# A graph attention network on one core: a third of the columns summed on TensorE, ScalarE three rows ahead, a new order of products and tiles

## The chip, the cores and the metric

The kernel runs on one core of one Trainium2 chip. The metric is the device time of one execution in microseconds; the kernel before took 6460.51 us, the median of three runs (6455.24 to 6466.45). A core has five engines that each work through their own queue in order and wait for each other by semaphores: TensorE (PE; PEld are its weight loads), VectorE (DVE), ScalarE (ACT), GpSimd (POOL) and SyncE (SP). Bulk data moves by DMA, started from a queue of SP, ACT or POOL.

## The reference, cut to what matters

There are 10000 nodes with 768 features and 170000 edges (80000 random pairs in both directions and a loop at each node), sorted by destination. Two layers of graph attention are computed, with 4 heads of 256 columns in the first and one head of 768 columns in the second:

```python
xl = (x @ W).reshape(n, heads, out_ch)
e = leaky_relu(alpha_src[src] + alpha_dst[dst], 0.2)
e = exp(e - segment_max(e, dst)[dst])
alpha = e / (segment_sum(e, dst)[dst] + 1e-16)
out = segment_sum(xl[src] * alpha[:, :, None], dst)
```

The kernel adds a loop of its own at every node, as the reference does. After layer 1: h1 = relu(layer_norm(out)) + x @ Wr1 + br1. After layer 2: h = layer_norm(out2) + h1 @ Wr2 + br2, and the result is layer_norm(x + h). All is float32.

## The kernel before, in words

**Preparation** (0 to 958 us). The rows x @ W1, with the two attention terms of each head appended, go to `table1` in DRAM, 1032 numbers a row. Beside that, `prepare` sorts the nodes by their number of in-edges and groups them into 79 tiles of 128 nodes. Tile t gets `SLOTS[t]` slots a node (its own row, then its in-edges, filled up with a row that has no weight). `slot_counts` (L54) fixes these numbers from a formula on the numbers of nodes and edges alone: 42 for tile 0, then 28, 27, 26, down to 11. `slots` holds the row number of each slot, and `FIRST[t]` is where tile t begins.

**The ring.** In both layers a tile is worked on slot by slot. `Ring` (L380) is a buffer in SBUF of 28 slots in layer 1 and 40 in layer 2; a slot holds one row of the table for each of the 128 nodes. `fetch` (L388) issues one indirect DMA from GpSimd for each slot, through `gather` (L364). It is called after each slot that was used, so that a slot is filled again as soon as it is free. A tile with more slots than the ring (the 42-slot tile alone) goes through `attend_parts` (L442) in three parts.

**Weights.** `logits` (L403) adds the terms, applies the leaky ReLU (L169), subtracts the maximum (L413, L416) and takes the exponential on ScalarE (L417). `normalised` (L420 to L426) divides by the sum.

**Layer 1** (`ordered_layer1`, L581), for each tile: logits; the statistics of the tile before (`deviation`: L473, L475 on VectorE, the square root at L477 on ScalarE); normalising; then ScalarE builds eight diagonal matrices from the weights of the first two slots (L619) and TensorE multiplies these slots' rows by them (L625), which starts the sum `acc` in PSUM. VectorE finishes h of the tile before (`scaled`: L483 to L485, and L635). TensorE transposes h (L491, copied out by ScalarE, L494). The remaining slots are added by `weigh`: of every three, the first is multiplied and added by VectorE alone (L439, four instructions of 256 columns), and the other two are multiplied in place by ScalarE (L433, four instructions) and added by VectorE (L435, 1024 columns). At fixed slots of this loop the larger products are issued (`dense`: h times W2 with its two attention columns, the product that becomes a row of `table2`, then x times Wr1), and near its end ScalarE copies the finished row (L651) and TensorE transposes x of the next tile. GpSimd then scatters the row to `table2` (L675). hT is stored to DRAM by SyncE (L643). Products and transposes share two PSUM buffers, `ps_big`, of two banks each; `acc` has two of its own.

**Layer 2** (`ordered_layer2`, L683), for each tile: `deviation` and `scaled` for the tile before, logits, the residual added (L722), normalising, a second `deviation`; then TensorE computes the residual x + h1 @ Wr2 of this tile (L740 with the identity, L742), and VectorE adds all slots over all 768 columns (L439). `finish` (L730 to L733) gives the last norm at the third slot, and GpSimd scatters the result (L758). hT and x of tile t+2 are asked for at the end of tile t (L704 on SyncE's queue, L364 on GpSimd's).

The order of each engine's instructions is the order of the program text; nothing reorders them (`tc.manual_schedule()`).

Of the kernel before, what the change touches and what calls it, by code (L numbers as in the profile page):

```python
# [41 lines left out]
G = 4  # L42
RING1 = 28
RING2 = 40
ON_PE1 = 2
# [8 lines left out]
def slot_counts(n_nodes, n_edges):  # L54
# [8 lines left out]
    for t in range(-(-n_nodes // P)):  # L63
        room = t * P if t else 0.002
        k = next((k for k, m in enumerate(tails) if m + 4.0 * math.sqrt(m) * (t > 0) <= room), DEGREES - 3)
        counts.append(min(k + 1, DEGREES - 2))
# [4 lines left out]
def gnn_kernel(ctx, tc, x, x_cols, src, dst, src_col, dst_col, W1, a_src1, a_dst1, b1, g1, be1, Wr1, br1,  # L71
# [13 lines left out]
    FIRST = [sum(SLOTS[:t]) for t in range(NT)]  # L85
# [12 lines left out]
    ps_big = ctx.enter_context(tc.tile_pool(name="ps_big", bufs=2, space=PSUM))  # L98
    ps_tr = None

    @contextmanager
    def psum_for_transposes():

        nonlocal ps_tr
        with tc.tile_pool(name="ps_tr", bufs=2, space=PSUM) as ps_tr:
            yield
# [8 lines left out]
    slots = consts.tile([P, FIRST[-1] + SLOTS[-1]], I32, name="slots")  # L115
# [29 lines left out]
    def product(aT, w, n):  # L145

        k = w.shape[1]
        p = ps_big.tile([P, 2 * BANK], F32, name="big")
# [231 lines left out]
    class Ring:  # L380
# [6 lines left out]
        def fetch(self, upto):  # L387
            for q in range(self.issued, min(upto, FIRST[-1] + SLOTS[-1])):  # L388
                gather(self.slot(q), self.table[:, :], slots[:, q:q + 1])
                self.issued = q + 1  # L390
# [36 lines left out]

    def weigh(acc, row, e, dh, first=None, shared=False):

        if shared:  # L430
            for h in range(e.shape[1]):
                s = slice(h * dh, (h + 1) * dh)
                nc.scalar.activation(row[:, s], row[:, s], AF.Copy, scale=e[:, h:h + 1])  # L433
# [8 lines left out]
    def attend_parts(small, ring, acc, h_, ad, bias, heads, dh, t):  # L442
# [6 lines left out]
        for lo, hi in zip(cuts, cuts[1:]):  # L449
# [13 lines left out]
            for q in range(lo, hi):  # L463
                weigh(acc, ring.slot(q), e[:, q - lo], dh, shared=heads > 1 and (q - lo) % 3)
# [48 lines left out]
    with tc.tile_pool(name="w1", bufs=1) as w1p, tc.tile_pool(name="l1", bufs=2) as io, \  # L513
            psum_for_transposes(), tc.manual_schedule():
# [65 lines left out]

    def ordered_layer1():  # L581
        with tc.tile_pool(name="b1", bufs=1) as pool, tc.tile_pool(name="small1", bufs=2) as small, \
                tc.tile_pool(name="ps_acc1", bufs=2, space=PSUM) as ps_acc, tc.manual_schedule():
            ring = Ring(pool, table1, R1, RING1)
            ring.fetch(RING1)

            def fetch_x(t):
                xt = pool.tile([P, D0], F32, name="xt", bufs=2)
                gather(xt, x[:, :], order[:, t:t + 1])
                return xt  # L590

            xs = {t: fetch_x(t) for t in range(min(2, NT))}
            g1_b, be1_b = (spread(pool, v, n) for v, n in ((g1, "g1"), (be1, "be1")))

            def transposed_x(t):
                to = pool.tile([P, K0, P], F32, name="xT", bufs=2)
                return to, columns(to, xs[t])

            xT, moves = transposed_x(0)
            last = None  # L600
            for t in range(NT + 1):
                live, events = t < NT, []
                whole = live and SLOTS[t] <= ring.size
                n = SLOTS[t] if live else 0
                if live:
                    acc = ps_acc.tile([P, 2 * BANK], F32, name="acc")
                if whole:
                    ad = ring.slot(FIRST[t])[:, C1 + H1:]
                    e, _ = logits(small, ring, FIRST[t], FIRST[t] + n, ad, H1, C1)
                if last:  # L610
                    h, r, mean_rows = last
                    stats = deviation(small, mean_rows, C1)
                if whole:
                    normalised(small, e, H1)

                    diagonals = pool.tile([P, ON_PE1 * H1, P], F32, name="diagonals")
                    for k in range(ON_PE1):
                        for i in range(H1):
# [415 lines left out]
```

## Time and profile before

| what | value |
|---|---|
| median of 3 runs | 6460.51 us (6455.24 to 6466.45) |
| the profiled execution | 6474.16 us, its span 6472.3 us |
| mean granted TensorE clock | 0.819 |
| busy, whole span | PE 65%, PEld 35%, DVE 78%, ACT 42%, POOL 55% |
| gathers into the ring (L364) | 2940, mean 949 ns on POOL |
| layer 2 rows on VectorE (L439, 768 columns) | 1392, mean 1022 ns |
| layer 1 rows on VectorE alone (L439, 256 columns) | 1856, mean 490 ns |
| layer 1 rows multiplied by ScalarE (L433) | 3400, mean 500 ns |
| and added by VectorE (L435, 1024 columns) | 850, mean 1233 ns |
| moved by DMA | 1666 MB, mean 257 GB/s |

The profile is of one execution. Its page gives the busy time of each engine; a view by stretches splits that by time; the timeline lists an engine's instructions with their start, their duration and, in brackets, the idle time before them and what ended it. Three stages can be told apart: preparation until 958 us, layer 1 until the first gather of layer 2 at 3974 us, and layer 2 until the end. VectorE's last row of layer 1 ends at 3942 us; between that and 3974 us lie the last tile's h, its product, its row and the scatter to `table2`. In layer 2 VectorE begins its work on tiles at 4034 us, and its first tile (42 slots) lasts until 4095 us; its last row ends at 6452 us.

### The profile page before, as it was taken

The page shows a single profiled execution, that of the slowest core. Times are in us where ns is not written, and L with a number is a line of the kernel's source. Part 1 is how long each engine was busy: PE and PEld are TensorE (multiplying, and loading weights), DVE is VectorE, ACT ScalarE, POOL GpSimd, SP SyncE. Part 2 cuts the span into 40 slices and gives each one's busy share as a digit, 9 for nine tenths or more (in the row PEclk, how much of TensorE's full clock was granted, in tenths as well). Part 3 has the DMA queues.
Part 4 walks back from the last instruction along what each step waited for, and adds up shares of the span by engine and source line. Part 5 has one row for each costly group of instructions (what it writes and reads, how often), then busy time and mean ns, then how long its engine had stood idle before and what let it go on. Part 6 is the DMA issues. An engine that isn't in the chain of part 4 may idle for free. (4 is left out here: it accounts for less than half of the span.)

```text
span 6472.3 us, 48744 instructions
## 1 busy us (share of the span) xinstructions
PE 4198.2 (65%) x11636; PEld 2278.5 (35%) x11636; DVE 5053.9 (78%) x8160; ACT 2688.0 (42%) x6591; POOL 3534.4 (55%) x3582
## 2 busy tenths in 40 slices
PE   8997982556766777778888996333434444445555
PEld 3443431333434444444455553111212222222332
DVE  5861426888888888888888884888878888888888
ACT  3433434666666666667666772011111111111111
POOL 3426534555555555555555553666666666666663
PEclk9999996778888888889899998666667777777777
DMA  4323237888888888888888885888878888888884
GB/s 140 122 76 70 93 106 287 289 293 315 299 301 301 303 304 297 300 295 299 293 299 307 308 312 180 277 281 288 281 272 287 282 280 281 279 286 283 279 291 161
DMA packets 459455, 1666.17 MB, mean 257 GB/s; under 512 B 105739, under 2 KB 109899, under 8 KB 459158
## 3 DMA queue, kind: packets, MB, share of 16 engines
q0 software_dynamic: 362176, 1486.59, 66.6%
q1 hardware_dynamic: 93168, 170.98, 7.8%
q10 hardware_dynamic: 3814, 5.39, 0.3%
q8 instruction: 94, 1.54, 0.1%
q14 instruction: 203, 1.66, 0.1%
HBM read 1516.88 MB, written 146.19 MB: 257 GB/s over the span
## 5 line engine op out<-in xcount | busy, mean ns | idle before, releaser
L364 POOL DMA_INDIRECT ring<-table,slots x2940 | 2789.2, 949 | 2161.4 <-DVE acc L439 889.7
L439 DVE SCALAR_TENSOR_TENSOR acc<-ring,e,acc 128x256 f32<-128x256 f32 (+1 forms) x3248 | 2332.4, 718 | 363.5 <-PE acc L625 201.5
L433 ACT ACTIVATE ring<-ring,e 128x256 f32<-128x256 f32 x3400 | 1390.8, 500 | 0.0
L435 DVE TENSOR_TENSOR acc<-acc,ring 128x1024 f32<-128x1024 f32 x850 | 1048.0, 1233 | 91.9 <-ACT ring L433 2.6
L740 PE MATMUL big<-wr,ident 128*128 128x512 f32 (+1 forms) x316 | 206.7, 745 | 1280.2 <-DMA wr<-in_x_dram,order 633.2
L742 PE MATMUL big<-w,wr 128*128 128x512 f32 (+1 forms) x2528 | 950.4, 531 | 23.1 <-issue 23.0
L625 PE MATMUL acc<-ring,diagonals 128*128 128x256 f32 x1248 | 424.3, 514 | 698.9 <-ACT diagonals L619 586.8
L152 PE MATMUL big<-w,hT 128*128 128x512 f32 (+1 forms) x2528 | 840.2, 490 | 56.8 <-ACT hT L494 56.8
L152 PE MATMUL big<-w,xT 128*128 128x512 f32 x1896 | 833.4, 601 | 55.8 <-DMA xT<-in_x_cols_dram 34.7
L152 PE MATMUL big<-wr,xT 128*128 128x512 f32 x1896 | 829.5, 594 | 0.7 <-ACT xT L494 0.7
L742 PEld LDWEIGHTS big<-w,wr 128*128 128x128 f32 x2528 | 531.3, 210 | 468.1 <-issue 432.6
L477 ACT ACTIVATE sd<-mv,eps 128x1 f32<-128x1 f32 x237 | 69.7, 294 | 1358.1 <-issue 585.4
L152 PEld LDWEIGHTS big<-w,hT 128*128 128x128 f32 x2528 | 471.9, 189 | 411.8 <-issue 289.1
L625 PEld LDWEIGHTS acc<-ring,diagonals 128*128 128x128 f32 x1248 | 326.9, 269 | 782.7 <-ACT diagonals L619 598.2
L152 PEld LDWEIGHTS big<-w,xT 128*128 128x128 f32 x1896 | 363.3, 193 | 522.9 <-issue 501.8
L740 PEld LDWEIGHTS big<-wr,ident 128*128 128x128 f32 x316 | 69.7, 249 | 1349.3 <-issue 449.3
L152 PEld LDWEIGHTS big<-wr,xT 128*128 128x128 f32 x1896 | 360.8, 190 | 423.4 <-issue 417.7
L417 ACT ACT_TABLE_LOAD x156 | 200.1, 1283 | 717.7 <-DVE e L416 636.7
L569 DVE TENSOR_TENSOR scr<-big,as_b 128x1024 f32<-128x1024 f32 x79 | 96.7, 1224 | 441.2 <-ACT row L566 426.3
L574 POOL TENSOR_TENSOR row<-row,none 128x1024 f32<-128x1024 f32 x79 | 187.0, 2368 | 334.9 <-ACT row L566 334.3
L572 ACT ACTIVATE scr<-scr 128x256 f32<-128x256 f32 x632 | 253.4, 402 | 122.2 <-DVE scr L569 118.3
L477 ACT ACT_TABLE_LOAD x157 | 201.4, 1283 | 229.7 <-DVE mv L475 149.5
(146 smaller groups left out, 3359.3 us busy)
## 6 DMA issues: line engine op xcount, KB each, us to landing
ring<-table,slots POOLq DMA_INDIRECT x2940
table<-row SPq DMA_DIRECT2D x79, 516.0 KB
h_d<-hT SPq DMA_DIRECT2D x79, 512.0 KB
wr<-h_d SPq DMA_DIRECT2D x79, 512.0 KB
xT<-in_x_cols_dram SPq DMA_DIRECT2D x79, 384.0 KB
w<-in_W_dram SPq DMA_DIRECT2D x6, 512.0 KB
w<-in_W_dram SPq DMA_DIRECT2D x1, 3072.0 KB
wr<-in_Wr_dram SPq DMA_DIRECT2D x1, 3072.0 KB
```

Source lines behind the costliest of these rows:

```text
L152: nc.tensor.matmul(p[:, c:e], aT[:, j, :], w[:, j, c:e], start=(j == 0), stop=(j == k - 1))
L364: nc.gpsimd.indirect_dma_start(out=to, out_offset=None, in_=table, in_offset=bass.IndirectOffsetOnAxis(ap=index, axis=0), **more)
L417: nc.scalar.activation(e, e, AF.Exp)
L433: nc.scalar.activation(row[:, s], row[:, s], AF.Copy, scale=e[:, h:h + 1])
L435: nc.vector.tensor_add(acc[:, :c], acc[:, :c], row[:, :c])
L439: nc.vector.scalar_tensor_tensor(acc[:, s], row[:, s], e[:, h:h + 1], (acc if first is None else first)[:, s], op0=OP.mult, op1=OP.add)
L477: nc.scalar.activation(sd, mv[:, 1:2], AF.Sqrt, bias=eps)
L572: nc.scalar.activation(m[:, s], m[:, s], AF.Copy, accum_out=row[:, C1 + i * H1 + h:C1 + i * H1 + h + 1])
L574: nc.gpsimd.tensor_add(row[:, :C1], row[:, :C1], b1_b)
L625: nc.tensor.matmul(acc[:, c:d], diagonals[:, k * H1 + i, :], ring.slot(FIRST[t] + k)[:, c:d], start=(k == 0 and c % BANK == 0), stop=(k == ...
L740: nc.tensor.matmul(r[:, c:d], ident, xt[:, c:d], start=True, stop=False)
L742: nc.tensor.matmul(r[:, c:d], hT[:, j, :], wr2[:, j, c:d], start=False, stop=(j == K1 - 1))
```

## The change

1. **Slots.** The formula in `slot_counts` takes a binomial spread where it took a Poisson one. It gives 1456 slots in all instead of 1470: one less in ten tiles and two less in the two smallest. 42 and 28 stay.
2. **Tile order.** Both layers run from the tile with the fewest in-edges (9 slots) to the one with the most (42 slots, now last, in parts). The ring first fetches the first tile's slots, then x, then the rest.
3. **Layer 1, shares.** Of every four slots after the first two (`SHARE = 4`) VectorE has one alone and shares three with ScalarE, where it was one and two of three. ScalarE's multiplications are issued `LEAD = 3` slots ahead of VectorE's additions.
4. **Layer 1, weights ahead.** `weights_of(t + 1)` (logits, then normalising, diagonals and the first two slots' products) is issued in the last three slots of tile t, where the next tile's slots and three more fit the ring (up to 25 slots). For larger tiles it comes at the start of the tile.
5. **Layer 1, order of products.** At the start of a tile ScalarE multiplies ahead and copies the row of two tiles before (`store`), TensorE transposes x, VectorE finishes h of the tile before, TensorE transposes h and multiplies x by Wr1 (into a PSUM buffer of its own, `ps_r`); h times W2 follows after the fifth slot. Transposes and h times W2 share one buffer, `ps_h1`.
6. **Layer 2, columns.** VectorE sums columns 0 to 511 (`ON_PE2 = 512`). For columns 512 to 767 ScalarE builds a diagonal for each slot and TensorE multiplies the slot's columns by it (`sums`), the first half of the slots before `scaled`, the second half after the second `deviation`, both ahead of the residual. `acc` gets two buffers.
7. **Layer 2, order.** Weights of the next tile come in the last three slots, as in layer 1. hT and x of the next tile are asked for in the middle of the tile. The constant br1 @ Wr2 is computed after the first tile's residual, not before all tiles.

The core of the diff ("+" lines, shortened):

```diff
-        k = next((k for k, m in enumerate(tails) if m + 4.0 * math.sqrt(m) * (t > 0) <= room), DEGREES - 3)
+        k = next((k for k, m in enumerate(tails)
+                  if m + 4.0 * math.sqrt(m * (1.0 - m / n_nodes)) * (t > 0) <= room), DEGREES - 3)
...
+    SLOTS, FIRST = SLOTS[::-1], FIRST[::-1]
...
+            def weights_of(t):
+                n = SLOTS[t]
+                e, _ = logits(small, ring, FIRST[t], FIRST[t] + n, ring.slot(FIRST[t])[:, C1 + H1:], H1, C1)
+                yield e
+                normalised(small, e, H1)
+                acc = ps_acc.tile([P, 2 * BANK], F32, name="acc")
+                diagonals = pool.tile([P, ON_PE1 * H1, P], F32, name="diagonals")
...
+                yield acc
...
+                if whole:
+                    e, acc = ready
+                    multiplied(ON_PE1 + LEAD)
+                if full is not None:
+                    store(t - 2)
...
+                    xT = pool.tile([P, K0, P], F32, name="xT")
+                    moves = columns(xT, xs[t])
+                if last:
+                    r, mean_rows = last
+                    h = pool.tile([P, C1], F32, name="h")
+                    scaled(h, mean_rows, C1, deviation(small, mean_rows, C1), g1_b, be1_b)
+                    nc.vector.scalar_tensor_tensor(h, h, 0.0, r[:, :C1], op0=OP.max, op1=OP.add)
+                for move in moves:
+                    move()
+                if last:
+                    hT = pool.tile([P, K1, P], F32, name="hT")
+                    events = [(ON_PE1 + j, move) for j, move in enumerate(columns(hT, h))]
+                if live:
+                    r = product(xT, wr1, C1, ps_r)
...
+                for k in range(n if whole else 0):
+                    multiplied(k + 1 + LEAD)
+                    if k >= n - LEAD:
+                        ready += itertools.islice(ahead, 1)
+                    if k >= ON_PE1:
+                        weigh(acc, ring.slot(FIRST[t] + k), e[:, k], DH1, shared=shared(k))
+                    ring.fetch(FIRST[t] + k + 1 + ring.size)
+                    due(k)
...
+            def sums(t, acc, e):
+                n = SLOTS[t]
+                nc.tensor.matmul(acc[:, ON_PE2:C2], ones, b2_b[0:1, ON_PE2:], start=True, stop=False)
+                for k in range(n):
+                    if k == n // 2:
+                        yield
+                    if k % G == 0:
+                        diagonals = pool.tile([P, G, P], F32, name="diagonals", bufs=2)
+                    nc.scalar.activation(diagonals[:, k % G, :], ident, AF.Copy, scale=e[:, k, :])
+                    nc.tensor.matmul(acc[:, ON_PE2:C2], diagonals[:, k % G, :],
+                                     ring.slot(FIRST[t] + k)[:, ON_PE2:C2], start=False, stop=(k == n - 1))
...
+                    for k in range(n if whole else 0):
+                        if k >= n - LEAD:
+                            ready += itertools.islice(ahead, 1)
+                        weigh(acc, ring.slot(FIRST[t] + k), e[:, k], ON_PE2, None if k else b2_b)
+                        ring.fetch(FIRST[t] + k + 1 + ring.size)
+                        if last and k == 1:
+                            finish()
...
+                        if t + 1 < NT and k == n // 2:
+                            ins[t + 1] = fetch_x(t + 1)
```

## The prediction, made before the changed kernel was built or run

> **What bounds the kernel now.** I read the time by stretches first, then the timeline of each engine around the end of one tile, once in layer 1 and once in layer 2. The stretches (us, then busy time of PE, PEld, DVE, ACT, POOL, then clock, DMA share, GB/s):
>
> ```profile
> 975.00:3960.00 2985.00, 2198.47 (x6761) 1287.44 (x6762) 2520.34 (x3969) 1983.05 (x4735) 1521.78 (x1614) 0.86 0.83 294
> 3960.00:6445.00 2485.00, 1132.39 (x2894) 610.92 (x2892) 2036.12 (x3171) 347.35 (x476) 1576.34 (x1627) 0.72 0.82 277
> 965.00:995.00 30.00, 0.00 (x0) 0.00 (x0) 1.98 (x6) 0.00 (x0) 22.68 (x25) 0.50 1.03 415
> ```
>
> VectorE is the busiest engine in both layers. DMA is not the limit: its share of 0.83 goes with 294 GB/s, but while the first ring fills it moves 415 GB/s. In layer 1, VectorE over one tile boundary:
>
> ```profile
> 2423.52 1.23 DVE L435 TENSOR_TENSOR acc<-acc,ring 128x1024 f32<-128x1024 f32 x1
> ...
> 2428.45 1.28 DVE L483 SCALAR_TENSOR_TENSOR h<-acc,mv,g 128x1024 f32<-128x1024 f32 x1
> 2429.64 0.15 DVE L484 RECIPROCAL sd<-sd 128x1 f32<-128x1 f32 x1
> ...
> 2431.22 1.22 DVE L635 SCALAR_TENSOR_TENSOR h<-h,big 128x1024 f32<-128x1024 f32 x1
> 2435.16 2.06 DVE L439 SCALAR_TENSOR_TENSOR acc<-ring,e,acc 128x256 f32<-128x256 f32 x4 [2.72 <-PE acc L625]
> ```
>
> From the last row (ends 2424.66) to the next tile's first (2435.16) is 10.5 us, 2.7 of them a wait for TensorE's two rows; all else is work. ScalarE at the same boundary:
>
> ```profile
> 2427.54 1.28 ACT L477 ACT_TABLE_LOAD   x1
> 2428.84 0.29 ACT L477 ACTIVATE sd<-mv,eps 128x1 f32<-128x1 f32 x1
> 2429.04 2.43 ACT L619 ACTIVATE diagonals<-ident,e 128x128 f32<-128x128 f32 x8
> ```
>
> Here the square root comes ahead of the diagonals, so VectorE never waits for it. In layer 2 (GpSimd, then VectorE):
>
> ```profile
> 5209.75 0.94 POOL L364 DMA_INDIRECT ring<-table,slots  x1 [8.75 <-DVE acc L439]
> 5211.00 0.95 POOL L364 DMA_INDIRECT ring<-table,slots  x1 [0.30 <-issue]
> 5212.25 0.94 POOL L364 DMA_INDIRECT ring<-table,slots  x1 [0.30 <-issue]
> ```
> ```profile
> 5211.77 16.89 DVE L439 SCALAR_TENSOR_TENSOR acc<-ring,e,acc 128x768 f32<-128x768 f32 x16
> 5262.26 1.02 DVE L483 SCALAR_TENSOR_TENSOR wr<-acc,mv,g 128x768 f32<-128x768 f32 x1 [1.19 <-DVE mv L475]
> 5265.76 1.02 DVE L485 SCALAR_TENSOR_TENSOR wr<-wr,sd,be 128x768 f32<-128x768 f32 x1 [2.41 <-issue]
> 5267.86 0.19 DVE L409 TENSOR_TENSOR e<-ring,ad 128x19 f32<-128x19 f32 x1 [1.01 <-DVE ad L718]
> 5268.56 0.18 DVE L169 SCALAR_TENSOR_TENSOR e<-e 128x19 f32<-128x19 f32 x1 [0.52 <-DVE e L409]
> ```
>
> GpSimd issues a gather every 1.25 us and has little slack. VectorE takes 1.056 us a row, and in stretches starts instructions only at multiples of 0.70 us, for no reason that the profile names. Added up over the layer these stretches leave it idle for 297 us, 3.8 us a tile; layer 1 has none.
>
> **What the skill says.** "ScalarE: Activation LUTs", section "What ACT_TABLE_LOAD costs": every switch between function sets loads a table, about 1283 ns. The trace has 1283 ns each, two a tile. "TensorE: Matmul & The Clock Gate", Part 1: the clock is at half rate until TensorE has been busy for some 3.4 us, and falls back when idle. The trace agrees: granted clock 0.50 where no matmul runs; 512-column products start 0.85 us apart at first, then 0.43. "Runtime: NRT & Kernel Launch", "Instruction fetch mechanics": fetching is mostly hidden. That speaks against it as the cause of the 0.70 us stretches, but no run here shows either.
>
> **Layer 1, part by part.** The slot formula gives 1470 rows before and 1456 after; the 42-row tile is one of 79. On the other 78 the rule k-2 mod 3 gives 449 rows to VectorE alone and 823 to ScalarE plus VectorE; mod 4 on the new lists gives 344 and 914. From the timeline, start to start, the first kind takes 2.17 us and the second 1.30. Check of before: 78 x 10.5 + 449 x 2.17 + 823 x 1.30 = 2863; with 76 for the 42-row tile from 1004 this ends at 3943, and the trace ends at 3942.
>
> Fixed part after: logits, exp and normalising move among the last three rows of the tile before, and TensorE's rows are done before they are needed, so the 2.7 us wait goes. What is late next is the square root. ScalarE's queue after normalising (time 0) is now: 8 diagonals 2.4, two rows ahead (8 x 0.41 = 3.3), row copy 0.75, table load 1.28, square root 0.3, done at 8.1. VectorE has two rows left (3.0 mean), statistics 1.5 and one pass 1.28, so it stands at its reciprocal at 5.8: it waits **2.3 us**. Behind the waiting square root stand xT's copies and the next rows' multiplies, which have slack: ScalarE needs 4.95 us for three rows where VectorE takes 6.07 for the four. Exp is also less covered, +0.2. Fixed part 10.5 - 2.7 + 2.3 + 0.2 = 10.3, taken as 10.2. Sum: 78 x 10.2 + 344 x 2.17 + 914 x 1.30 = 2730.
> Small tiles meet another loop: h, transposes 1.1, product r 10.4, product with w2 10.6, cold clock about 2.5 (an estimate from 5.6 us for 16 matmuls that warm take 3.6), row copy, load, root, the last two passes 2.7: 29.5 us. Tiles of up to 14 rows are shorter than that: +44.
> Large tiles: before, logits waited 5.4 us at most for a row whose slot had been freed some 1.5 us earlier, so freed to landed is about 6.5 us. Logits three rows earlier are exposed by 6.5 - 1.52 x (25 - n): 47 us in all for tiles of up to 25. The three larger ones keep their waits (17) and run logits and all else in series (15).
> The start: before, the first weighing was at 1004, behind ScalarE's wait for x; with 9 rows fetched first it is near 978. Sum: 978 + 2730 + 44 + 79 + 86 (the 42-row tile, now last, with its boundary) = 3917 against 3942; the closing chain gains 2 for the division. **Layer 1: -23 us.**
> GpSimd's store waits there for the row copy, with the next gathers behind it; its 25.9 us a tile leave room. TensorE's one remaining buffer for transposes and the w2 product makes a chain (row copy, x, h, product), which lies inside the 29.5 us loop and costs nothing above 14 rows; uncovered it would cost up to 3 us a tile, as in (a) with the other sign. SyncE's store of hT keeps its place.
>
> **Layer 2, part by part.** VectorE takes 512 of 768 columns: 256 columns 0.490, 768 columns 1.022 (by form), so 512 about 0.756 (an estimate on that line), 0.79 start to start: 0.265 less on 1414 rows. In proportion to the wide row it would be 0.68, to the narrow one 0.98; I take the line through both, since both are measured. Each 0.05 is 71 us where VectorE leads. Fixed: from 5228.70 to 5235.83 is 7.1, plus finish 0.34. Added: the root now needs a load after exp (+0.6), and exp is less covered (+0.85): 8.9. With 3.8 for the slow stretches, a tile costs 12.7 + 0.79 n. TensorE: 256 columns cost 2 x 0.226 = 0.45 warm, 0.86 cold; n + 1 of them, plus the residual 12.4 to 15.0: at n = 18, 21 to 24 us beside VectorE's 26.9, hidden with some 3 us to spare. ScalarE: n diagonals at 0.30 (8 took 2.43), 424 us on an engine busy 347 of 2485. GpSimd: 1.253 n + 2.6 (x and out), 25.2. Where cover is gone TensorE's excess adds one to one, as it holds the ring's slots. x and hT for the next tile are asked for in mid-tile instead of two tiles ahead: at least 20 us before use, hidden.
> Sum over tiles of the larger of VectorE and GpSimd: 2122 (GpSimd ahead on 15 tiles). Start after the first gather 23 (landing of the vectors, as the trace has for b2), last tile of 42 rows 62, end 22: 2229. Before: 6472 - 3974 = 2498. **Layer 2: -269 us.**
>
> Together -292; I take 12 back for variation between three engines within 10 per cent: span 6472 - 280 = 6192, in the profiled execution 6194 for its 6474.2 (1.9 us lie around the span). The median of runs is 13.7 lower than that execution, so 6460.5 - 280 = **6180**.
>
> **Rivals.** (a) More than forecast: ScalarE's square root isn't late (the load runs early, or rows are shorter) and VectorE's fixed part is 7.9: 78 x 2.3 = 179 less, 30 of it lost to TensorE's loop: 6030. For it: ScalarE has a third of the layer free; against: its queue is in order. Losing the slow stretches in layer 2 instead would bring 97 (2122 to 2025): 6083.
> (b) Gain given back: denser gathers lengthen the slow stretches or residuals come late, 1.8 us a tile: +140, 6320. For it: the stretches are found only in the layer where GpSimd issues without pause.
> (c) **Slower**: TensorE's sums start cold each tile and stay so, 0.86 a slot and residual 15.0; a tile takes the larger of that and VectorE, 2453 in sum, layer 2 = 2560, +62 - 23: 6500. It decides where a slot costs over about 0.82. For it: clock 0.72 in the layer; against: sums and residual lie closer together than anything there now.
> (d) The change doesn't act (waits of whole tiles keep the orders as before): 6460.
>
> **Chances.** Forecast 0.48 (own range 6110 to 6260), (a) 0.23, (b) 0.20, (c) 0.07, (d) 0.02. About 0.2% is what a measurement can tell from no change. Range 6000 to 6340, which leaves out (c) and the far ends. Faster 0.91, same 0.02, slower 0.07.
>
> **What would show it.** Layer 1: a wait of VectorE's reciprocal for ScalarE's root of about 2.3 us a tile and no wait for acc. Layer 2: 512-column rows near 0.76 us, a tile near 27 us, GpSimd busy over 90 per cent of the layer with its gathers' spacing counted, TensorE's 256-column matmuls at 0.23 each. Wrong: layer 1 shorter by over 100 us, or layer 2 by under 150.

## The result and the profile after

The changed kernel takes **6972.3 us** (median of 4 runs, 6969.5 to 6980.0), the kernel before 6457.9 in the same series: 8.0 per cent slower, ratio 1.080 [1.078, 1.083]. Layer 1 became shorter and layer 2 much longer. The border between them is GpSimd's first gather of layer 2:

| | first gather of layer 2 | layer 2 to the end |
|---|---|---|
| before (span 6472.3) | 3974.3 | 2498.0 |
| after (span 6972.1) | 3922.3 | 3049.8 |
| difference | -52 | +552 |

The stretches of after, in the columns of the first fence of the prediction:

```profile
975.00:3905.00 2930.00, 2233.56 (x6753) 1291.25 (x6754) 2434.08 (x3634) 2140.63 (x5111) 1517.39 (x1600) 0.88 0.85 297
3910.00:6950.00 3040.00, 1944.76 (x5873) 1311.50 (x5871) 1657.25 (x3159) 769.93 (x1888) 1555.91 (x1614) 0.80 0.66 225
```

In layer 2 VectorE has 380 us less work than before, but is now busy for only 55 per cent of the stretch; no engine is above 65. The layer waits. The view of the waits over layer 2 says for what (engine, tile and line that waits, then what it waits for; us in total, times, longest):

```profile
DVE acc L449 <- PE acc L782: 983.9, 77, 20.8
...
ACT diagonals L781 <- remote: 505.2, 60, 13.0
```

The first is VectorE's first row of a tile, which stands until TensorE's sums of the same tile are done: 77 times, 12.8 us each. The second is ScalarE, which stands at a diagonal for a buffer that TensorE has to free; "remote" is the profile's word where it finds no work that ended just then. One tile boundary of after, VectorE, ScalarE, TensorE and GpSimd (start, duration, then the instruction, in brackets the idle time before it):

```profile
5020.02 0.21 DVE L488 BATCH_NORM_AGGREGATE mv<-st 128x2 f32<-128x12 f32 x1
5033.17 0.76 DVE L449 SCALAR_TENSOR_TENSOR acc<-ring,e,b 128x512 f32<-128x512 f32 x1 [12.95 <-PE acc L782]
```
```profile
5015.93 2.43 ACT L781 ACTIVATE diagonals<-ident,e 128x128 f32<-128x128 f32 x8
5021.25 0.29 ACT L490 ACTIVATE sd<-mv,eps 128x1 f32<-128x1 f32 x1 [2.89 <-DVE mv L488]
5026.91 2.44 ACT L781 ACTIVATE diagonals<-ident,e 128x128 f32<-128x128 f32 x8 [5.37 <-remote]
```
```profile
5016.37 5.71 PE L782 MATMUL acc<-ring,diagonals 128*128 128x256 f32 x16 [5.09 <-issue]
5027.37 5.77 PE L782 MATMUL acc<-ring,diagonals 128*128 128x256 f32 x18 [5.29 <-ACT diagonals L781]
```
```profile
5021.50 0.95 POOL L370 DMA_INDIRECT ring<-table,slots  x1 [0.30 <-issue]
5022.75 1.01 POOL L861 DMA_INDIRECT out_dram<-out,order  x1 [0.30 <-issue]
5034.20 0.97 POOL L370 DMA_INDIRECT ring<-table,slots  x1 [10.44 <-DVE acc L449]
```

TensorE ends its first eight sums at 5022.08. ScalarE, which needs the first of their two groups of diagonals back, goes on only at 5026.91. TensorE then ends the sums at 5033.14, and VectorE begins 0.03 us later. GpSimd, whose ring slots come free with VectorE's rows, stops in between.

The trace also records the updates of semaphores. Here they are around that moment as time:number; 108 is raised by TensorE, 101 by VectorE, 110 by ScalarE, 111 to 118 by the gathers:

```
5020.49:104  5021.16:101  5021.87:108  5021.88:117  5022.60:118  5023.26:118
5024.02:111  5024.75:112  5025.34:112  5026.07:113  5026.08:108  5026.77:114
5026.78:114  5026.80:108  5026.85:108  5026.89:108  5026.93:108  5026.95:114
5026.96:114  5026.97:108  5027.02:108  5027.02:114  5027.06:108
```

While GpSimd issues gathers one behind the other, an update comes every 0.70 us, as if they stood in one line. 2.3 us after the end of GpSimd's last issue (the store at 5022.75) the line is worked off at once, and in it are eight of TensorE's updates (5026.08 to 5027.06) for matmuls that had ended by 5022. That the way of an update to the other engines lies outside the span that the profile gives an instruction is stated by the Trainium skill in "Perfetto Trace Analysis", section "Per-instruction lifecycle: what the profiler-reported window actually captures"; it has no figure for it. Here it is over 4 us. I call such updates late, and a stretch of over 3.5 us with updates 0.5 to 0.9 us apart a **train** (updates a few hundredths of a microsecond apart count as one). After has 521 us of trains, before 713, nearly all in layer 2. These sums are rough: if no updates are counted as one, they are 345 and 424. Nor do they give a cost, since before has more of them than after; only large differences between them are used below. In before, VectorE's slow starts fall on updates of its own semaphore (5255.23:101 5256.63:101 5258.03:101 5259.43:101, between them gathers' updates): so the multiples of 0.70 us look like late updates too.

So two theories. **A**: VectorE's first row waits for TensorE's sums because both fill one PSUM tile, `acc`, and the sums take longer than VectorE's own work at the boundary. **B**: while GpSimd issues gathers back to back, what one engine reports to another arrives late; the change has put several such hand-overs in a row into every tile.

### The profile page after: what moved, and what is told of

It is laid out like the page before. It is cut to its first block, busy times and chain, and to the rows that moved or that the text cites. A ratio compares the mean times of both kernels' runs of the same rounds, so it can differ in the third digit from the quotient of the medians.

```text
span 6972.1 us, 57674 instructions
## 1 busy us (share of the span) xinstructions
PE 5045.9 (72%) x14620; PEld 2983.5 (43%) x14620; DVE 4585.1 (66%) x7812; ACT 3267.8 (47%) x8379; POOL 3508.3 (50%) x3554
## 5 line engine op out<-in xcount | busy, mean ns | idle before, releaser
L449 DVE SCALAR_TENSOR_TENSOR acc<-ring,e,acc 128x256 f32<-128x256 f32 (+2 forms) x2802 | 1748.2, 624 | 101.2 <-remote 14.5
L782 PE MATMUL acc<-ring,diagonals 128*128 128x256 f32 x2828 | 956.9, 513 | 970.3 <-ACT diagonals L781 521.6
L438 ACT ACTIVATE ring<-ring,e 128x256 f32<-128x256 f32 x3776 | 1530.8, 500 | 0.0
L782 PEld LDWEIGHTS acc<-ring,diagonals 128*128 128x128 f32 x2828 | 740.0, 268 | 1186.6 <-ACT diagonals L781 561.0
L445 DVE TENSOR_TENSOR acc<-acc,ring 128x1024 f32<-128x1024 f32 x944 | 1162.9, 1232 | 81.8 <-ACT ring L438 9.6
L158 PE MATMUL big<-wr,xT 128*128 128x512 f32 x1896 | 910.7, 640 | 19.1 <-ACT xT L507 19.1
L793 PE MATMUL big<-w,wr 128*128 128x512 f32 (+1 forms) x2528 | 844.0, 486 | 8.0 <-issue 8.0
L781 ACT ACTIVATE diagonals<-ident,e 128x128 f32<-128x128 f32 x1414 | 442.6, 388 | 618.0 <-remote 505.2
L449 DVE SCALAR_TENSOR_TENSOR acc<-ring,e,b 128x512 f32<-128x512 f32 x78 | 59.3, 760 | 999.4 <-PE acc L782 983.9
L634 PE MATMUL acc<-ring,diagonals 128*128 128x256 f32 x1248 | 336.9, 431 | 316.1 <-ACT diagonals L629 316.1
L634 PEld LDWEIGHTS acc<-ring,diagonals 128*128 128x128 f32 x1248 | 269.1, 219 | 379.4 <-ACT diagonals L629 299.3
L504 PE MATMUL big<-ident,h 128*128 128x128 f32 x632 | 129.9, 374 | 320.1 <-DVE h L685 293.9
```

The source lines that it names most:

```text
L158: nc.tensor.matmul(p[:, c:e], aT[:, j, :], w[:, j, c:e], start=(j == 0), stop=(j == k - 1))
L445: nc.vector.tensor_add(acc[:, :c], acc[:, :c], row[:, :c])
L449: nc.vector.scalar_tensor_tensor(acc[:, s], row[:, s], e[:, h:h + 1], (acc if first is None else first)[:, s], op0=OP.mult, op1=OP.add)
L504: nc.tensor.transpose(p[:, i, :], a[:, i * P:(i + 1) * P], ident)
L634: nc.tensor.matmul(acc[:, c:d], diagonals[:, k * H1 + i, :], ring.slot(FIRST[t] + k)[:, c:d], start=(k == 0 and c % BANK == 0), stop=(k == ...
L781: nc.scalar.activation(diagonals[:, k % G, :], ident, AF.Copy, scale=e[:, k, :])
```

## Experiments

**e1_split**: the sums in a PSUM tile of their own.

```
-                    acc = ps_acc.tile([P, 2 * BANK], F32, name="acc")
-                    tail = sums(t, acc, e)
+                    acc = ps_acc.tile([P, BANK], F32, name="acc")
+                    side = ps_side.tile([P, BANK], F32, name="side")
+                    tail = sums(t, side, e)
```
(statistics and scaling read the two tiles in turn: 3 statistics of 256 columns, two scalings)

> Layer 2's sum is kept in two PSUM tiles, one that VectorE alone writes (512 columns) and one that TensorE alone writes (256); three statistics instructions instead of two and one more pass, about 0.5 us a tile. Theory A (VectorE's first row of a tile waits for TensorE's sums only because both write one tile): the wait of 12.8 us a tile on 77 tiles goes, layer 2 falls from 3050 us to 2250 to 2350, the whole to 6200 to 6350 us. Rival B (TensorE's chain of sums and residual is itself too long, some 30 us a tile, because its completions are seen late): VectorE then waits for the residual or for the sums at the statistics instead, and the whole stays above 6600 us.

6607.6 us, ratio 1.022 [1.020, 1.024]. The wait of the first row is gone, and 365 us with it, but VectorE now waits at the next thing that it needs of TensorE, the residual:

```profile
DVE wr L843 <- remote: 446.9, 44, 14.2
```

A is a part of it and not the whole.

**e2_no_sums**: VectorE takes all 768 columns again; everything else of the change stays.

```
-ON_PE2 = 512
+ON_PE2 = 768
-                    tail = sums(t, acc, e)
+                    tail = iter(())
```

> VectorE sums all 768 columns in layer 2 and TensorE none; the order is else that of the changed kernel. Theory A: the wait of the first row goes with TensorE's sums; a tile costs VectorE 12.7 + 1.056 n, layer 2 about 2590 us, the whole about 6510 us. If the new order of layer 2 itself costs the time (weights ahead, later fetches), it stays near 6900 us.

6409.3 us (a single run; before 6466.8 in its series), 100 less than expected. Layer 2 runs from 3923.8 to 6406.9, 2483 against 2498 before: what else was changed in layer 2 is worth 15 us, and giving columns to TensorE costs the 563 between this kernel and the changed one, although it takes 380 us of work from VectorE.

**e3_sums_early**: all sums ahead of the scaling instead of half of them.

```
-                    if k == n // 2:
-                        yield
...
+                yield
```

> Both halves of TensorE's sums are issued ahead of the normalisation of the tile before, so that ScalarE's second square root no longer stands between the diagonals. Theory A with the order on ScalarE as the cause of late sums: the sums end some 4 us earlier a tile, 6650 to 6750 us. Rival B (completions of TensorE are seen late, and ScalarE's ninth diagonal waits for them whatever the order): VectorE's second root is now queued behind that wait; 6900 to 7050 us.

6948.9 us (a single run): the order on ScalarE isn't it. The wait moved into the sums themselves ("remote" at the diagonals 619 us over the stretch to 6400).

**e4_diagonals**: seven buffers for groups of four diagonals instead of two, so that ScalarE needs nothing back from TensorE within a tile.

```
-                        diagonals = pool.tile([P, G, P], F32, name="diagonals", bufs=2)
+                        diagonals = pool.tile([P, G, P], F32, name="diagonals", bufs=7)
```

> Seven groups of four diagonals instead of two, so that ScalarE builds a tile's diagonals without waiting for TensorE. ScalarE idles 505 us before diagonals in the changed kernel. If that wait is what delays the sums: 450 us less, about 6530 us, and VectorE's first row still waits some 5 us a tile. If TensorE would be late without it too: above 6850 us.

6676.6 us (a single run), between the two. This one hand-over cost 296 us; with it gone, the first row still waits 573 us up to 6400.

**e5_both**: e1_split with five groups of diagonals (`bufs=5`).

> This is the change with both suspected causes taken away together: the sums of TensorE in a PSUM tile of their own (as in e1_split) and five groups of diagonals in place of two (as in e4_diagonals, which had seven). Theory (two causes that add up: VectorE's first row waits for all of TensorE's sums, and the hand-over of diagonals between ScalarE and TensorE is seen late): e1_split gained 364 us and e4_diagonals 297 us of the change's 6972, so both give 6300 to 6400, and ScalarE's 277 us of 'remote' waits at its diagonals go; the residual add of VectorE, which waited 710 us in e1_split, waits under 350. Rival (the two gains are one and the same wait, counted twice): 6550 to 6610.

6585.8 us, ratio 1.020 [1.018, 1.022]: the rival held. The two gains, 365 and 296, are not a sum; VectorE waits for the residual as in e1_split (735 us up to 6400). The trains are there (561 us).

**e6_residual_first**: as e5_both, the residual ahead of the sums.

```
                     side = ps_side.tile([P, BANK], F32, name="side")
+                    r_next = residual(t)
                     tail = sums(t, side, e)
...
-                    r = residual(t)
+                    r = r_next if whole else residual(t)
```

> As e5_both, and the residual's product of a tile stands ahead of the tile's sums on TensorE instead of behind them, so that VectorE, which adds it one tile later, has a whole tile for a late update to arrive. Theory (lateness costs only where a hand-over has no slack): VectorE is left with its own work, some 1540 us in layer 2 and some 5 us a tile of short waits, or the gathers become the bound; 6150 to 6300. Rival (the gathers of layer 2 bound it whatever the order, since their rows come free late or their updates are late too): as e2_no_sums, 6370 to 6450.

6664.8 us, ratio 1.033 [1.031, 1.034]: neither. VectorE's wait at the residual is gone, but two waits that nobody had counted come last (over the stretch to 6400):

```profile
ACT out L854 <- DMA out_dram<-out,order: 662.1, 52, 17.2
PE big L792 <- DMA wr<-in_x_dram,order: 577.8, 57, 13.1
```

TensorE stands at the residual for x, which is asked for in the middle of the tile before and stands in GpSimd's queue; ScalarE stands at the output because its one buffer is still to be stored.

**e7_paced** and **e8_half_rows** ask what makes the updates late: GpSimd's issuing, or the bytes. e7 is the changed kernel with

```
                 gather(self.slot(q), self.table[:, :], slots[:, q:q + 1])
+                if self.pause is not None:
+                    nc.gpsimd.memset(self.pause, 0.0)
```
(`pause` a tile of 128x512, in layer 2 alone), e8 the changed kernel with

```
-                gather(self.slot(q), self.table[:, :], slots[:, q:q + 1])
+                gather(self.slot(q)[:, :self.width], self.view, slots[:, q:q + 1])
...
+            ring.width, ring.view = R2 // 2, table2[:, :].rearrange("n (h c) -> (n h) c", h=2)
+            nc.vector.memset(ring.rows[:, :, ring.width:], 0.0)
```

e8 leaves the right half of every row out and so does not compute the graph's result; it serves the time alone.

> The change as it is, with one memset of 128x512 by GpSimd behind every gather of layer 2, so that gathers can no longer follow each other every 1.25 us. Theory (GpSimd's issuing of gathers back to back makes the updates of semaphores late): the trains of updates 0.70 us apart (521 us in the change) fall under 200 us, ScalarE's 505 us of 'remote' waits at its diagonals fall under 200, and the kernel is faster than 6973: 6600 to 6850. Rival (the traffic of the transfers makes them late, not the issuing): trains of 400 us or more and 6900 to 7100.

> The change as it is, but each gather of layer 2 brings 385 columns in place of 770: the same number of gathers and of 128 pieces each, half the bytes. It leaves the right half of each row out (set to zero once), and the rows fetched are not those of the graph. Theory (GpSimd's issuing makes the updates late): the trains stay at 400 us or more, the 'remote' waits stay over 350 us and the time is 6850 to 7050. Rival (the traffic of the bytes makes them late): trains under 200 us and 6500 to 6750.

e7 6669.4 us, e8 6973.2 (a single run each). In e7 everything fell as the theory had it; in e8 the time and the "remote" wait did, the trains did not. **Half the bytes change nothing in the time**: 131 GB/s over the stretch 3980 to 6400 instead of 225, and the time is that of the changed kernel to 1 us. Its trains are 191 us, which the theory had at 400 or more and the rival under 200. But the recorded updates are as few (below), and ScalarE's "remote" wait up to 6400 is 374 us, 397 in the changed kernel. I take it that the measure of trains fails here and not the theory. **A memset that does nothing makes the kernel 303 us faster**: trains 8 us, no "remote" wait left at the diagonals. GpSimd, and VectorE at the same tile:

```profile
5007.62 0.95 POOL L370 DMA_INDIRECT ring<-table,slots  x1 [0.17 <-issue]
5009.28 0.95 POOL L370 DMA_INDIRECT ring<-table,slots  x1 [0.17 <-issue]
```
```profile
5000.33 0.21 DVE L490 BATCH_NORM_AGGREGATE mv<-st 128x2 f32<-128x12 f32 x1
5006.36 0.76 DVE L451 SCALAR_TENSOR_TENSOR acc<-ring,e,b 128x512 f32<-128x512 f32 x1 [5.83 <-PE acc L785]
```

A gather every 1.66 us instead of 1.25, and GpSimd is never idle: it is the bound now. The wait for the sums has fallen from 12.8 us a tile to 6.5 (494 us in 76 tiles up to 6500): half of it was late updates, half is A. What e7 spaces out is GpSimd's issuing and, with it, all that the gathers set off, their updates above all; e8 leaves both as dense as they were. Which of the two makes updates late, no run here separates.

**e9_short_pause** is e7 with a `pause` of 128x128, **e10_early_inputs** is e6 with

```
-                        diagonals = pool.tile([P, G, P], F32, name="diagonals", bufs=5)
+                        diagonals = pool.tile([P, G, P], F32, name="diagonals", bufs=4)
-                    o = pool.tile([P, C2], F32, name="out")
+                    o = pool.tile([P, C2], F32, name="out", bufs=2)
-                        if t + 1 < NT and k == n // 2:
+                        if t + 1 < NT and k == 0:
                             ins[t + 1] = fetch_x(t + 1)
```

**e11_early_and_pause** is e10 with e9's pause, **e12_before_pause** the kernel before with e9's pause.

> The change as it is with a memset of 128x128 behind every gather of layer 2 in place of e7_paced's 128x512. In e7_paced GpSimd was never idle (a gather every 1.66 us, some 33 us a tile), and ScalarE's output waited 18 us a tile for a store that stood in GpSimd's queue. Theory (any instruction of GpSimd between two gathers lets the updates through, and e7_paced was bound by GpSimd's pace): about 1.35 us a gather, 18 gathers and two others in 27 us a tile; VectorE needs 27 to 28 with its wait for the sums; trains under 150 us; 6100 to 6300. Rival (it takes the free time, 0.7 us a gather, and not just any instruction): trains over 300 us and 6750 to 6950.

> As e6_residual_first, with the two waits that were late there taken away: two buffers for the output (ScalarE waited 662 us for the store out of the only one) and the inputs of the next residual fetched behind the first row instead of halfway through a tile (TensorE waited 578 us for them); four groups of diagonals instead of five. Nothing is done about the late updates. Theory (the late updates turn up wherever the next hand-over has no slack): trains stay over 400 us, 6350 to 6550. Rival (slack at every hand-over is enough, lateness itself costs nothing): 6100 to 6300.

> As e10_early_inputs, with the memset of 128x128 behind every gather of layer 2. Theory: the updates come in time and every hand-over has slack; what is left is GpSimd's 27 us a tile (77 tiles: 2080), VectorE's 22 or the transfers, whichever is longest: 6000 to 6150. Rival (a memset of 0.2 us isn't enough to let the updates through): trains over 300 us and within 60 us of e10_early_inputs.

> The kernel before as it is, with the memset of 128x128 behind every gather of layer 2. Theory (VectorE's stretches of 0.70 us between instructions, 297 us in all, are late updates of its own semaphore while GpSimd issues gathers back to back): the trains (713 us) fall under 150 us, VectorE's short waits go, and 200 to 300 us of the 6455 go with them: 6150 to 6270. Rival (VectorE's stretches come from something else, or the memsets delay the gathers by as much): 6400 to 6500.

Measured: e9 6285.2 (ratio 1.018 [1.017, 1.020]), e10 6080.6 (a single run), e11 6195.8 (1.004 [1.003, 1.006]), e12 6280.8 (1.018 [1.016, 1.020]). But **the kernel before took 6169.9 here, not 6455**. The runs had fallen on another chip, and on it there is no train without a pause either (e10: 0 us). So none of the four tests B, whichever range its time fell into, and their times stand only against 6169.9. I say first kind for the chips of the result and of e1 to e8, second kind for this one. In all, three chips of the first kind (e1 to e4, e5 to e8, and that of e13, e14 and e18) and two of the second were met in the experiments.

What it shows instead: on a chip without trains the kernel before is 285 us faster; the prediction had read 297 us of slow stretches from its trace. That the two are the same is argued, since no trace of before itself was taken on this kind. Its layer 1 is as long on both kinds (e12's first gather of layer 2 is at 3975.0, that of before at 3974.3); that of the changed kernel is 8 to 12 us shorter on the second (3909.8 in e16 below, 3922.3 and, in e13, 3917.6 on the first). The number of updates that the trace holds between 4000 and 6000 us tells the kinds apart:

| kernel | chip | all updates | those of gathers |
|---|---|---|---|
| before | first | 5788 | 3739 |
| after | first | 7447 | 4185 |
| e8_half_rows | first | 7146 | 3464 |
| e7_paced | first | 24218 | 17414 |
| e10_early_inputs | second | 32419 | 24537 |
| after (e16, below) | second | 29903 | 22642 |

On the second kind a gather has some 16 updates; on the first most of them are not in the trace, unless GpSimd pauses; whether they were merged or only not recorded can't be told from it. The trace of before says the same without any pause: between 2000 and 3800 us, in layer 1, where an indirect transfer is issued every 1.80 us on average, 13.3 of the 16 are recorded for each; between 4000 and 6000, at one every 1.49 us, 2.8, although layer 1 moves more bytes (294 against 277 GB/s). It is the pace that differs.

**e13_change_again** (the changed kernel as it is) and **e14_early_inputs_again** (e10 as it is):

> The changed kernel as it is. On the chip of e9_short_pause to e12_before_pause the kernel before took 6170 us instead of 6455 and the trains of late updates were gone, in e10_early_inputs too, where GpSimd makes no pause; so what the change does without late updates has not been seen. If before is near 6170 here as well: theory (late updates make the change slow; without them only VectorE's wait for the sums is left, some 6 us a tile) 6150 to 6290; rival (the shared PSUM tile alone makes it slow) over 6350. If before is near 6455: 6950 to 6990, and nothing new.

> e10_early_inputs once more, for an interval. If before is near 6170: 6070 to 6095. If before is near 6455 (late updates): theory (late updates turn up wherever the next hand-over has no slack) 6350 to 6550; rival (slack at every hand-over is enough) 6080 to 6300.

These fell on the first kind (before 6459.4). e13: 6965.2, nothing new. e14: **6397.0, ratio 0.990 [0.989, 0.992]**, 316 us more than the same kernel on the other kind. The theory's 6350 to 6550 held: with slack given to the hand-overs that had been found, updates are still late somewhere. In its trace TensorE itself is held up, one matmul at a time, where it otherwise runs 16 of these in 3.6 us (506 us of trains in all):

```profile
5419.54 0.38 PE L794 MATMUL big<-w,wr 128*128 128x256 f32 x1 [1.31 <-issue]
5420.95 0.38 PE L794 MATMUL big<-w,wr 128*128 128x256 f32 x1 [1.04 <-issue]
5423.75 0.59 PE L794 MATMUL big<-w,wr 128*128 128x256 f32 x1 [2.42 <-issue]
```

The starts are 1.4 and 2.8 us apart, multiples of 0.70.

**e15_early_and_pause_again** (e11 as it is) and **e16_change_third** (the changed kernel as it is):

> e11_early_and_pause once more: e10's order and buffers with a memset of 128x128 by GpSimd behind every gather of layer 2. If before is near 6455 here (late updates): theory (an instruction of GpSimd between two gathers lets the updates through, so that with it both kinds of chip give the same time) 6180 to 6250, trains under 50 us, against the 6397 of e14_early_inputs_again; rival (0.2 us of memset isn't enough) 6350 or more with trains over 300 us. If before is near 6170: 6190 to 6200 again, nothing new.

> The changed kernel as it is, for the case that before is near 6170 here: theory (the late updates make it slow, and without them VectorE's wait for the sums is left, some 6 us a tile) 6150 to 6290; rival (the shared PSUM tile alone makes it slow) over 6350. If before is near 6455: 6950 to 6990, and nothing new.

Second kind (before 6169.1). e15: 6198.9, 1.005 [1.003, 1.007], nothing new. e16 is what was missing: **the changed kernel takes 6277.9 without late updates, ratio 1.018 [1.016, 1.019]**. It is slower there too, by 109 us instead of 506. A's wait stands alone:

```profile
DVE acc L449 <- PE acc L782: 504.7, 77, 11.5
```

One boundary shows why (VectorE, ScalarE, TensorE):

```profile
5412.61 0.18 DVE L432 TENSOR_TENSOR e<-e,total 128x20 f32<-128x20 f32 x1
...
5419.87 0.21 DVE L488 BATCH_NORM_AGGREGATE mv<-st 128x2 f32<-128x12 f32 x1
5427.46 0.76 DVE L449 SCALAR_TENSOR_TENSOR acc<-ring,e,b 128x512 f32<-128x512 f32 x1 [7.38 <-PE acc L782]
```
```profile
5415.59 0.29 ACT L490 ACTIVATE sd<-mv,eps 128x1 f32<-128x1 f32 x1 [2.58 <-DVE mv L488]
5415.79 2.43 ACT L781 ACTIVATE diagonals<-ident,e 128x128 f32<-128x128 f32 x8
```
```profile
5416.22 11.20 PE L782 MATMUL acc<-ring,diagonals 128*128 128x256 f32 x40 [7.41 <-ACT diagonals L781]
```

The weights are ready at 5412.79. The first diagonal stands behind a square root that waits for VectorE's statistics: 3.0 us. The 40 passes of the 20 rows take 11.2. VectorE's own work from 5412.79 is done at 5420.08, 7.3 us; the sums take 14.6. The rest is the wait.

The sums begin at half clock, after TensorE's 7.4 us of idling. The stretches of this boundary, in the columns of the first fence of the prediction, the seventh number being the granted clock:

```profile
5416.00:5421.00 5.00, 4.78 (x12) 3.85 (x12) 3.87 (x7) 3.17 (x12) 3.78 (x5) 0.51 1.00 388
5421.00:5427.00 6.00, 6.00 (x29) 5.27 (x28) 0.00 (x0) 3.06 (x10) 3.09 (x4) 1.00 0.95 335
```

Up to 5421 a pass starts every 0.43 us, then every 0.22. In all of e16, 640 of 2733 such distances are near 0.43 us, some 8 a tile; at 0.22 they would take 1.8 us a tile less (an estimate from these figures). So the cold start is a part of A's wait of 6.6 us, and the smaller one.

That the wait is what makes the changed kernel slower on this kind fits e10, which has no such wait and takes 6080.6; but e10 differs in several things, and e1 alone was not run on it.

**e17_before_pause_again** (e12 as it is):

> e12_before_pause once more: the kernel before with a memset of 128x128 by GpSimd behind every gather of layer 2. If before is near 6455 here (late updates): theory (VectorE's 297 us of stretches with an instruction every 0.70 us are late updates, and GpSimd's pause lets them through) about the 6281 of the other kind of chip: 6260 to 6310, trains under 50 us against 713; rival (0.2 us of memset isn't enough) 6400 to 6480 with trains over 400 us. If before is near 6170: 6276 to 6285 again, nothing new.

Second kind again (before 6170.4): 6283.9, 1.019 [1.017, 1.020]. Whether a memset of 0.2 us frees the kernel before of its trains on the first kind was not seen. What e12 and e17 show is the price of a pause where nothing is late. A gather comes every 1.33 us instead of 1.25: 0.08 on 1470 gathers are 118 us, and the kernel is 111 and 114 slower. e11 against e10 gives 115. So GpSimd's queue was near its limit in before and in e10 on that kind, as far as these sums tell; in the changed kernel, which waits anyway, the same pause costs 7 (e9 against e16).

**e18_tiny_pause**: e11 with a `pause` of one column.

> As e10_early_inputs, with a memset of a single column (128x1, about 0.1 us on GpSimd) behind every gather of layer 2, where e11_early_and_pause has 128x128. If before is near 6455 here (late updates; e14_early_inputs_again took 6397): theory (any instruction of GpSimd between two gathers lets the updates through) 6080 to 6200 with trains under 100 us; rival (what helps is free time, as e7_paced's 0.5 us) 6330 or more with trains over 300 us. If before is near 6170 (e10_early_inputs took 6081, e11_early_and_pause 6196): the memset costs its time in GpSimd's queue or nothing, 6075 to 6130; rival (GpSimd isn't the bound and the memset of 0.2 us costs by something else) 6170 to 6200.

First kind (before 6459.2): 6417.5, ratio 0.995 [0.993, 0.997]; trains 562 us. The rival held: the memset of 0.11 us falls into the gap of 0.30 that is there anyway (in the timeline gathers start at 5005.89, 5007.14 and 5008.39), so that they still follow each other every 1.25 us, and the updates stay late. It is time between gathers that lets them through, not an instruction, as far as e7 (built on the changed kernel) and e18 (built on e10) can be compared.

## Why the prediction was wrong

Forecast 6180, measured 6972: by its own steps,

- **Layer 1, -23 us forecast, -52 measured.** The mechanism was right. The reciprocal waits for the square root as forecast at 2.3 us:

```profile
2435.88 0.17 DVE L497 RECIPROCAL sd<-sd 128x1 f32<-128x1 f32 x1 [1.85 <-ACT sd L490]
```

1.85 in this tile, 2.6 in the mean (199.8 us, 77 times), and no wait for `acc` is left. The fixed part of that tile is 10.1 us (7.6 from last row to first, 2.5 of logits and normalising among the last rows), forecast 10.2. Waits for landing rows are 49 us, forecast 64. The start gave less: first weighing at 996.5, forecast 978. I did not trace the other 30 us to a term. No experiment did layer 1 alone.
- **The 512-column row, 0.756 us forecast, 0.755 measured.** The line through the two known widths held, and VectorE's work in layer 2 fell as it should.
- **"TensorE ... hidden with some 3 us to spare": this is the step that failed.** It set TensorE's work of a tile (21 to 24 us) beside VectorE's (26.9). Both are busy times. But VectorE's first row needs the end of all the sums, since they share `acc`, and the sums can't begin before the weights: they had to fit into the 7 us of VectorE's boundary, not into its 27 us tile. They take 14.6 from the weights on, 3.0 of it behind the square root; a row of 256 columns costs TensorE 0.56 us there (11.2 for 20), not 0.45, because the first ones run at half clock. Without late updates that is 505 us (e16), 6.6 a tile.
- **The slow stretches, "3.8 us a tile", kept as they were: the second step that failed.** They were late updates, found in before where VectorE follows itself; the raster in its trace and the 285 us between the kinds of chip say so, a run of before with pauses on the first kind was not made. How much they cost depends on how many hand-overs stand in a row. If all that the two kinds of chip differ by is put down to them, late updates cost before 305 us in layer 2 (2498 against 2193 on the second kind, an estimate with the border at 3975 as in e12) and after 681 (3050 against 2369, border at 3910). That difference, 376, and the 176 that are left without late updates, A's wait among them, make the +552. On a chip of the first kind alone, e7 shows at least 303 of the 681. The layer took 821 us more than the forecast of 2229: 140 without late updates, and 681 with them. That fetching is mostly hidden, as the Trainium skill has it in "Runtime: NRT & Kernel Launch", section "Instruction fetch mechanics", was cited against one cause; no run contradicts it, but ruling out one cause named none.
- **What there was to gain was small.** On the second kind layer 2 of before takes 2193 us, less than the 2229 that was forecast for after. e10 brings it to 2168 (6079 - 3911). GpSimd's gathers alone, 1456 x 1.253 + 79 x 2.6, are 2030 of that. The forecast saw GpSimd ahead on 15 tiles; it is the limit of the layer once VectorE isn't.
- **Rivals.** (b) named the mechanism, "denser gathers lengthen the slow stretches or residuals come late", and priced it at 140 us where late updates alone cost 376 us more in after than in before. (c) is half right: the sums start cold, in 69 of e16's 77 tiles and 66 of after's, but they don't stay so. A slot cost 0.56 us in e16's tile and 0.64 to 0.71 in the tile of after shown above (5.77 us for 18 passes, 5.71 for 16, two passes a slot), under the 0.82 that (c) needs; the clock in the layer rose from 0.72 to 0.80. What made them costly was not the sum of TensorE's work, as (c) has it, but the wait for its end. The chance of 0.07 for slower had only this one mechanism in it. (a), a square root that isn't late, did not come.
- **Its own signs.** The forecast had named a layer 2 shorter by under 150 us as a sign of being wrong; it became 552 longer. A tile of 17 slots takes 34.1 us from first row to first row (4999.08 to 5033.17) where 27 was expected.

A version that beats both kernels on both kinds is e10: 0.990 [0.989, 0.992] on the first, 6081 against 6170 in a single run on the second (0.986). On the second kind most of that is layer 1. On the first, a longer pause of GpSimd in it might give more, since e7's took the trains away; that was not run there.

Open: why chips differ and in what else, what serves the updates every 0.70 us, whether GpSimd's issuing or the number of updates fills that line, whether a pause helps the kernel before on the first kind, and whether a pause between 0.1 and 0.5 us is enough on the first kind.

## What to carry to other kernels

Work that is handed to an idle engine is hidden only if its way from the last input to the first use, with all that stands ahead of it in each queue, is shorter than what the waiting engine has to do meanwhile; compare these two stretches and not busy times, price the first work of an engine that has been idle at the slow clock that its trace shows, and give the result a buffer of its own so that it is needed late. A wait that the profile puts down to "remote", or starts that fall on a fixed raster, deserve an answer before the change is priced: they may grow with every hand-over that is added. Repeat the kernel before beside every experiment, since the same pair of kernels differed by 8.0 per cent on one chip and by 1.8 on another.

## What the hardware showed that I had not expected

- On three of the chips in these runs, updates of semaphores came one per 0.70 us while GpSimd issued gathers every 1.25 us: over 4 us late in the tile shown, those of several engines in one line, TensorE's matmuls held up as well (e14). On two others there was none of it in the traces (e10, e16: 0 us of trains), and the same kernel was 285 us (before) to 694 us (after) faster.
- The time did not depend on the bytes: rows of half the width gave 6973.2 against 6972.3 us. A memset of 0.54 us between gathers took the trains away (8 us for 521), a memset of 0.11 us in the existing gap did not (562).
- After 7.4 us of idling TensorE's passes of 256 columns started every 0.43 us for some 5 us, at a granted clock of 0.51, and every 0.22 us after that (e16).
